# A recommender's attention kernel: four transpose banks, attention as columns, tail chunks spread, one shared PSUM bank

## The chip, the cores and the metric

The kernel runs on one core of a Trainium2 chip. The metric is the device time of one execution in microseconds, as the median of several runs; lower is better. The core has five engines that work side by side and wait for each other by semaphores: TensorE (PE; its weight loads are listed as PEld), VectorE (DVE), ScalarE (ACT), GpSimd (POOL) and SyncE (SP). PE writes its results to PSUM[...].

## The reference: what is computed

For each of 16384 samples, 69 user fields and one label are looked up in a table of 100001 rows of 96 numbers. Each looked-up row `u` gets one attention number from a small network that sees it beside the label's row `q`; the rows, weighted by it, are summed in ten groups of fields; a three-layer network makes one number of the result.

```
u  = emb[batch_user]                      # 16384 x 69 x 96
ql = emb[batch_label[:, 0]]
z  = concatenate([q, u, q - u, q * u])    # q: ql repeated over the fields
h  = dice(z @ W1 + b1, a1)                # 64 hidden numbers
att = (h @ W2 + b2) @ W3 + b3             # one number per sample and field
pre = where(batch_user < 100000, u * att, 0)
pooled = einsum('gf,bfe->bge', window, pre)      # groups of 20,20,10,10,2,2,2,1,1,1 fields
x = concatenate([pooled, ql])
h = dice(bn(x @ Wf1 + bf1)); h = dice(bn(h @ Wf2 + bf2)); return h @ Wf3 + bf3
# dice(x, a) = (a * (1 - p) + p) * x, p = sigmoid(bn(x))
```

All of it is in float32.

## The kernel before

**Tiling.** The samples are cut into 32 blocks (`NBLK`) of 512. A block's lookups are cut into 69 chunks of 512 rows. The first 64 chunks (main chunks) hold eight samples each with their first 64 fields; the last five (tail chunks, `NTAIL`) hold all 512 samples of the block with one field each (65 to 69), whose group sums are trivial. `chunk_of` (L64) says which chunk of which block has the running number c. Two chunks make a pair; there are 1104 pairs (`NPAIR`).

**One pair's way.** `fetch` (L361) gathers eight tiles of 128 rows by indirect DMAs on POOL (`gather`, L267; tile `u`, 17 buffers), turns each by a PE transpose into a PSUM bank `ptr` (pool `ps_tr`, two banks, L250), and DVE makes two copies of it: `uT` (L378), and `quT`, multiplied by the label's row (L381, or L388 for a tail chunk). `hidden` (L391) makes the hidden sums `ph` on PE and their sigmoid `y` on ACT; `product` (L411) finishes the dice on DVE. `attend_rows` (L417), once every four pairs, multiplies the four `y` by `v2` (32 columns, two of them used), each into its own 32 partitions of one bank (`prow`), which ACT copies to `row`; `turn_band` (L433) turns that back with four transposes (`patt`), so that each row of a chunk has its attention on its own partition; `weigh` (L443) makes the weights `rw` of it on DVE. `pool_sums` (L460) multiplies `rw` by the rows `u` on PE into one of three sets in the bank `acc` (L254), and `pool_copy` (L482) brings a set to `pooled` on DVE. A tail chunk has no pool sums: `attend_tail` (L426) multiplies directly.

**Rows that POOL doesn't gather.** One tile of 128 rows in each of 245 chunks is fetched row by row, by direct DMAs on SP's queue (109 chunks, `SP_CHUNKS`) and ACT's queue (136 chunks, `ACT_CHUNKS`), into a ring of seven buffers (`Singles`, L277; issues at L303). `scalar_rows` (L652) puts 16 ACT issues in each pair's step, behind the step's sigmoid.

**The top network.** `top_steps` (L561) cuts a block's top network into ten steps: four parts of the first layer for each of two halves (`top1`, L508), `top2` (L527), `top3` (L536). They have a PSUM bank of their own (`ps_m`, L255).

**Order.** The order is written out by hand (`manual_schedule`, L737): `plan` (L629) lists for step i what is issued, and each engine does its share in that order. In the main loop (L659 to L686) step i holds the hidden sums of pair i-2, 16 ACT row fetches, the pool sums of pair i-9 (`POOL_LAG`, L41), the product of pair i-3, the pooled copy of pair i-10, and then the fetch of pair i; every fourth step also the attention rows, the turning and the weights of four pairs. The last 16 pairs have an order of their own (L688 to L707, L732 to L735). The labels of block n are gathered 14 steps before its first pair, turned 11 and applied 9 steps before (L714 to L716), and the top network of a block starts 13 steps after its last pair (L717 to L719). The pool `ps_x` (two banks) holds `prow`, `patt`, the labels' banks and the tail products.

Of the kernel before, what the change touches and what calls it, by code (L numbers as in the profile page):

```python
# [18 lines left out]
P = 128  # L19
# [21 lines left out]
POOL_LAG = 9  # L41
# [21 lines left out]

def chunk_of(c):  # L64

    n, k = divmod(c, NCH)
    if n == NBLK - 1 and k >= EARLY:
        k = NMAIN + k - EARLY if k < EARLY + NTAIL else k - NTAIL
    return n, k
# [47 lines left out]
def rec_kernel(  # L117
# [132 lines left out]
    ps_tr = ctx.enter_context(tc.tile_pool(name="ps_tr", bufs=2, space=PSUM))  # L250
    ps_h = ctx.enter_context(tc.tile_pool(name="ps_h", bufs=2, space=PSUM))
    ps_x = ctx.enter_context(tc.tile_pool(name="ps_x", bufs=2, space=PSUM))
    ps_acc = ctx.enter_context(tc.tile_pool(name="ps_acc", bufs=1, space=PSUM))
    acc = ps_acc.tile([E, 3, 2, NS, G], F32, tag="acc", name="acc")  # L254
    ps_m = ctx.enter_context(tc.tile_pool(name="ps_m", bufs=1, space=PSUM))  # L255


# [86 lines left out]
    def head_rows(n):  # L344

        for h in range(2):
# [86 lines left out]
    def turn_band(b, n):  # L433

        row = bands.pop(b)
        pt = ps_x.tile([P, 4, n, 32], F32, tag="x", name=f"patt{b}")
        for t in range(4):
            nc.tensor.transpose(  # L438
                pt[:, t].rearrange("p k j -> p (k j)"), row[:, t * P : (t + 1) * P], ident[0 : 32 * n, 0 : 32 * n]
            )  # L440
        turned[b] = pt

    def weigh(b, n):  # L443

        pt = turned.pop(b)
# [14 lines left out]
    def pool_sums(i):  # L460
# [6 lines left out]
        pa = acc[:, i % 3]  # L467
# [75 lines left out]
    def store(n):  # L543

        p4 = ps_x.tile([n, P], F32, tag="x", name="p4")
# [31 lines left out]
    def rows_of(b, n):  # L577
        return lambda: attend_rows(b, n)
# [236 lines left out]
```

## Time and profile before

| | |
|---|---|
| median of 3 runs | 10949.98 us (10947.27 to 10950.51) |
| the profiled execution's own time | 13684.32 us |
| its span, first to last instruction | 13682.6 us |
| mean granted TensorE clock | 0.72 |
| POOL: gathers of `u` + of labels | 8587 + 128, 944 and 946 ns each by their own span |
| DVE `uT` + `quT` (L378, L381) | 673 ns each, x2208 and x2048 |
| ACT copy `row` (L423) | 584 ns, x275 of 128 partitions |
| PE pool sums (L327, `acc`) | x15930 + 454, 269 ns each |
| PE transposes `patt` (L438) | x1108, 375 ns each |
| PE `prow` (L421) | x2208, 851 ns each |
| DMA | 458 MB, 34 GB/s |

The span is that of one execution under the profiler, which is 25% longer than the timed ones. PE's records count each float32 product as two instructions; the durations of overlapping matmuls overlap, so that their sum is more than PE's time. In the prediction's fences a timeline line gives start, duration, engine, line, operation, output and input tiles, count, and in brackets how long the engine sat idle before and what ended that. A group line gives count, busy time and mean, and after the second bar the idle time before the group. "issue" is idle time for which the profile shows no reason, "remote" a semaphore whose setter it can't name.

### The profile page before, as it was taken

What the parts mean: (1) busy time and instruction counts of PE and PEld (TensorE: products, weight loads), DVE (VectorE), ACT (ScalarE), POOL (GpSimd) and SP (SyncE); (2) the same over time, 40 slices, a digit from 0 to 9 for tenths busy, and PEclk for the clock granted to TensorE, in tenths of its full rate; (3) what the DMA queues carried; (4) which work ended last, traced back from release to release, by engine and by line L of the source; (5) the groups of instructions that cost most, each with busy time, mean ns of one, the idle gap of its engine ahead of it and who ended that gap; (6) DMA issues with size and microseconds to landing.
All of it is one profiled execution on the core that took longest, in us unless ns stands there. A gap on an engine that the chain in (4) does not pass through costs nothing.

```text
span 13682.6 us, 171148 instructions
## 1 busy us (share of the span) xinstructions
PE 9106.3 (67%) x41797; PEld 4711.6 (34%) x41797; DVE 5074.9 (37%) x8639; ACT 990.6 (7%) x1657; POOL 8225.3 (60%) x8721
## 2 busy tenths in 40 slices
PE   3666666666666666666776666666666666676668
PEld 1333333333333333333333333333333333333334
DVE  2333333333333333333333333333333333333333
ACT  0000000000000000000000000000000000000001
POOL 5666566656666656666665665665665666556663
PEclk7677776777767777677776777777777777777677
DMA  1111111111111111111111111111111111111111
GB/s 38 34 34 33 34 33 33 33 35 33 33 34 34 35 33 33 33 33 36 33 33 33 33 36 33 34 33 33 36 33 33 34 33 35 33 33 34 33 33 22
DMA packets 344459, 458.45 MB, mean 34 GB/s; under 512 B 202354, under 2 KB 202866, under 8 KB 343330
## 3 DMA queue, kind: packets, MB, share of 16 engines
q0 software_dynamic: 278880, 428.92, 15.0%
q1 hardware_dynamic: 29762, 11.82, 0.4%
q10 hardware_dynamic: 34816, 6.75, 0.3%
q8 instruction: 336, 5.51, 0.2%
q14 instruction: 665, 5.45, 0.1%
HBM read 446.74 MB, written 0.07 MB: 33 GB/s over the span
## 4 chain that ended last, share of the span: by engine, by line
PE 37%; issue 20%; another core or an unknown queue 18%; ACTq 12%; DVE 10%; POOL 2%; ACT 1%; DMA 0%; POOLq 0%
ACTq L303 10%; PE acc L327 8%; PE ph L401 6%; PE ptr L327 6%; PE ph L405 5%; PE p L521 5%; DVE uT L378 3%; DVE quT L381 2%; POOL u L268 2%; PE prow L421 2%; DVE y L415 1%; DVE y L414 1%; ACTq L288 1%; PE pa L430 1%
## 5 line engine op out<-in xcount | busy, mean ns | idle before, releaser
L268 POOL DMA_INDIRECT u<-in_rows,ids x8587 | 8103.5, 944 | 5290.9 <-issue 2228.3
L327 PE MATMUL acc<-rw,u 128*96 128x20 f32 x15930 | 1972.9, 269 | 1685.7 <-issue 1088.5
L489 DVE COPY pooled<-acc 96x160 f32<-96x160 f32 x1008 | 429.0, 426 | 6575.4 <-remote 4728.2
L327 PEld LDWEIGHTS acc<-rw,u 128*96 128x96 f32 x15930 | 1853.6, 201 | 2757.0 <-issue 1954.3
L327 PE MATMUL ptr<-ident,u 128*96 128x128 f32 x8587 | 1655.6, 341 | 866.1 <-issue 659.3
L378 DVE COPY uT<-ptr 96x512 f32<-96x512 f32 x2208 | 1485.9, 673 | 996.2 <-remote 756.4
L405 PE MATMUL ph<-quT,wn 96*64 96x512 f32 x4416 | 1625.1, 727 | 195.2 <-issue 189.6
L401 PE MATMUL ph<-uT,A 128*64 128x512 f32 x4096 | 1637.7, 830 | 156.9 <-issue 106.2
L327 PEld LDWEIGHTS ptr<-ident,u 128*96 128x96 f32 x8587 | 1250.6, 166 | 1082.2 <-issue 864.1
L381 DVE TENSOR_TENSOR quT<-ptr,qT 96x512 f32<-96x512 f32 x2048 | 1378.6, 673 | 0.0
L407 ACT ACTIVATE y<-ph 128x512 f32<-128x512 f32 x1104 | 658.6, 597 | 8853.1 <-remote 3304.5
L405 PEld LDWEIGHTS ph<-quT,wn 96*64 96x64 f32 x4416 | 447.3, 175 | 1257.0 <-issue 1255.2
L414 DVE SCALAR_TENSOR_TENSOR y<-y,na1c,ph 128x512 f32<-128x512 f32 x1104 | 810.3, 734 | 177.1 <-ACT y L407 97.0
L415 DVE SCALAR_TENSOR_TENSOR y<-ph,wn,y 128x512 f32<-128x512 f32 x1104 | 828.8, 751 | 39.4
L521 PE MATMUL p<-pooled,wf 96*100 96x512 f32 (+1 forms) x1400 | 713.8, 643 | 84.9 <-issue 82.0
L438 PE MATMUL patt<-ident,row 128*128 128x128 f32 x1108 | 259.5, 375 | 641.4 <-issue 274.9
L421 PE MATMUL prow<-y,v 128*32 128x512 f32 x2208 | 540.7, 851 | 115.0 <-issue 95.6
L401 PEld LDWEIGHTS ph<-uT,A 128*64 128x64 f32 x4096 | 279.0, 169 | 868.9 <-issue 783.3
L521 PE MATMUL p<-pre,V 96*100 96x512 f32 (+1 forms) x700 | 424.0, 745 | 140.4 <-issue 89.2
L438 PEld LDWEIGHTS patt<-ident,row 128*128 128x128 f32 x1108 | 185.1, 194 | 775.8 <-issue 554.0
L521 PEld LDWEIGHTS p<-pooled,wf 96*100 96x100 f32 x1400 | 251.0, 192 | 450.3 <-issue 450.0
L430 PE MATMUL pa<-y,vrep 64*96 64x512 f32 x320 | 231.3, 895 | 203.2 <-DVE pre L431 127.6
(72 smaller groups left out, 2682.1 us busy)
## 6 DMA issues: line engine op xcount, KB each, us to landing
ring<-in_rows ACTq DMA_DIRECT2D x17408, 0.4 KB
ring<-in_rows SPq DMA_DIRECT2D x13952, 0.4 KB
u<-in_rows,ids POOLq DMA_INDIRECT x8587
ids<-in_idx SPq DMA_DIRECT2D x8, 560.0 KB, 2.5
q<-in_emb,ids POOLq DMA_INDIRECT x128
wf<-in_far SPq DMA_DIRECT2D x1, 1209.0 KB
wn<-in_near SPq DMA_DIRECT2D x1, 236.0 KB, 3.1
ids<-in_idx SPq DMA_DIRECT2D x1, 140.0 KB
```

Source lines behind the costliest of these rows:

```text
L268: nc.gpsimd.indirect_dma_start(out=dst, out_offset=None, in_=table, in_offset=bass.IndirectOffsetOnAxis(ap=index, axis=0),)
L303: d = self.engine.dma_start(out=ring[r : r + 1, b], in_=row_bytes[:, bass.ds(self.values[r], ROW_BYTES)]).then_inc(self.sems[k], 16)
L327: ins = op(out, ring[:, at[0]].bitcast(F32) if at else u[:, 4 * (c % 2) + t, :], other, **how)
L378: nc.vector.tensor_copy(uT[j][0:E], ptr)
L381: nc.vector.tensor_tensor(quT[:, j, :].rearrange("e (s f) -> e s f", f=FM), ptr.rearrange("e (s f) -> e s f", f=FM), by_field(q[:, k * NS ...
L401: nc.tensor.matmul(p, As[n % 2][:, k // 4, :], uT[j], start=True, stop=False)
L405: nc.tensor.matmul(p, Wp, quT[:, j, :], start=False, stop=True)
L407: nc.scalar.activation(y, ph, AF.Sigmoid, scale=S_DICE)
L414: nc.vector.scalar_tensor_tensor(y, y, na1c, ph, ALU.mult, ALU.mult)
L415: nc.vector.scalar_tensor_tensor(y, ph, a1c, y, ALU.mult, ALU.add)
L421: nc.tensor.matmul(pr[32 * k : 32 * (k + 1), :], v2, ys[b + k], start=True, stop=True)
L521: nc.tensor.matmul(p1, w[:, h * DH : (h + 1) * DH], x, start=(k == 0), stop=(k == KTOP - 1))
```

## The change

In the pools: transposes get four banks; `ps_x` has one; the top network's bank `ps_m` goes, and its halves take `ps_x`; one bank `shared` holds two sets of pool sums, the attention columns of five bands of four pairs (`place`), and the last layer's result. In place of rows, copy and turning, `attend` multiplies each quarter of `y`, as the stationary operand, by the two used columns of `v2`: the attention comes out on the right partition at once, and `weigh` reads it from `shared`. The tail chunks of all blocks but the last stand at places 48, 53, 58, 63 and 68 of a block. Pool sums run ten steps behind in place of nine, labels are gathered 16 steps ahead, and the steps of the top network are placed anew.

```diff
-POOL_LAG = 9
+POOL_LAG = 10
...
+TAIL_AT = [48 + 5 * f for f in range(NTAIL)]
 def chunk_of(c):
     n, k = divmod(c, NCH)
-    if n == NBLK - 1 and k >= EARLY:
-        k = NMAIN + k - EARLY if k < EARLY + NTAIL else k - NTAIL
+    if n == NBLK - 1:
+        if k >= EARLY:
+            k = NMAIN + k - EARLY if k < EARLY + NTAIL else k - NTAIL
+    elif k in TAIL_AT:
+        k = NMAIN + TAIL_AT.index(k)
+    else:
+        k -= sum(at < k for at in TAIL_AT)
     return n, k
...
-    ps_tr = ctx.enter_context(tc.tile_pool(name="ps_tr", bufs=2, space=PSUM))
+    ps_tr = ctx.enter_context(tc.tile_pool(name="ps_tr", bufs=4, space=PSUM))
     ps_h = ctx.enter_context(tc.tile_pool(name="ps_h", bufs=2, space=PSUM))
-    ps_x = ctx.enter_context(tc.tile_pool(name="ps_x", bufs=2, space=PSUM))
+    ps_x = ctx.enter_context(tc.tile_pool(name="ps_x", bufs=1, space=PSUM))
     ps_acc = ctx.enter_context(tc.tile_pool(name="ps_acc", bufs=1, space=PSUM))
-    acc = ps_acc.tile([E, 3, 2, NS, G], F32, tag="acc", name="acc")
-    ps_m = ctx.enter_context(tc.tile_pool(name="ps_m", bufs=1, space=PSUM))
+    shared = ps_acc.tile([P, 512], F32, tag="shared", name="shared")
+    sets = shared[0:E, 0:320].rearrange("e (k j s g) -> e k j s g", k=2, j=2, g=G)
+    def place(b, n):
+        start = 320 + 32 * (b // 4 % 5) + 8 * (b % 4)
+        return shared[:, start : start + 8 * n].rearrange("p (t k j) -> p t k j", t=4, j=2)
...
-    def head_rows(n):
-        for h in range(2):
+    def head_rows(n, halves=(0, 1)):
+        for h in halves:
...
-    def attend_rows(b, n):
-        pr = ps_x.tile([P, 512], F32, tag="x", name=f"prow{b}")[0 : 32 * n]
-        for k in range(n):
-            nc.tensor.matmul(pr[32 * k : 32 * (k + 1), :], v2, ys[b + k], start=True, stop=True)
-        row = rpool.tile([P, 512], F32, tag="row", name=f"row{b}")[0 : 32 * n]
-        nc.scalar.copy(row, pr)
-        bands[b] = row
+    def attend(i, b, n):
+        out = place(b, n)
+        for t in range(4):
+            nc.tensor.matmul(out[:, t, i - b, :], ys[i][:, t * P : (t + 1) * P], v2[:, 0:2], start=True, stop=True)
...
-    def turn_band(b, n):
...
     def weigh(b, n):
-        pt = turned.pop(b)
+        pt = place(b, n)
...
-        pa = acc[:, i % 3]
+        pa = sets[:, i % 2]
...
-            banks, tag = (ps_h, "h") if n == NBLK - 1 and cols.start >= BLK // 2 and h == 1 else (ps_m, "m")
+            banks, tag = (ps_tr, "tr") if n == NBLK - 1 and h == 1 else (ps_x, "x")
...
-        p2 = ps_m.tile([D2, BLK], F32, tag="m", name=f"p2_{n}_{cols.start}")[:, cols]
+        p2 = ps_x.tile([D2, BLK], F32, tag="x", name=f"p2_{n}_{cols.start}")[:, cols]
...
-        p3 = ps_m.tile([P, k1 - k0], F32, tag="m", name=f"p3_{n}_{cols.start}")
+        p3 = shared[:, 480 + NQ * (n % 2) + k0 : 480 + NQ * (n % 2) + k1]
...
     for i in range(e):
-        if i >= 7 and i % 4 == 3 and i < e - 1:
-            at(i, rows_of(i - 7, 4))
         if i >= 4:
             at(i, tails_of(i - 4))
-        if i >= 8 and i % 4 == 0:
-            at(i, lambda b=i - 8: turn_band(b, 4))
         if i >= 2:
             at(i, sums_of(i - 2))
         at(i, lambda i=i: scalar_rows(i))
...
+        for k in [i - 5] if i < e - 1 else [i - 5, i - 4]:
+            if k >= 0:
+                at(i, lambda k=k: attend(k, k - k % 4, 4))
         if i >= 3:
             at(i, product_of(i - 3))
...
+        if i < e - 2:
+            if i >= POOL_LAG:
+                at(i, lambda k=i - POOL_LAG: pool_sums(k))
+            if i > POOL_LAG:
+                at(i, lambda k=i - POOL_LAG - 1: pool_copy(k))
...
         at(i, fetch_of(i))
-        if i >= 8 and i % 4 == 0:
-            at(i, lambda b=i - 8: weigh(b, 4))
+        if i >= 9 and (i - 9) % 4 == 0:
+            at(i, lambda b=i - 9: weigh(b, 4))
...
-            at(first - 14, lambda n=n: qs.__setitem__(n, head_gather(n)))
-            at(first - 11, lambda n=n: head_turn(n, qs.pop(n)))
-            at(first - 9, lambda n=n: head_rows(n))
-        if n < NBLK - 2:
-            for s, work in enumerate(top_steps(n, slice(0, BLK))):
-                at(end + POOL_LAG + 4 + s, work)
...
+            at(first - 16, lambda n=n: qs.__setitem__(n, head_gather(n)))
+            at(first - 13, lambda n=n: head_turn(n, qs.pop(n)))
+            at(first - 11, lambda n=n: head_rows(n, [0]))
+            at(first - 9, lambda n=n: head_rows(n, [1]))
+        steps = [12, 12, 13, 13, 15, 15, 16, 16, 18, 20] if n < NBLK - 2 else [12, 12, 12, 12, 13, 13, 13, 13, 18, 19]
+        if n < NBLK - 1:
+            for step, work in zip(steps, top_steps(n, slice(0, BLK))):
+                at(end + step, work)
```

The closing pairs keep their order, with `attend` in the place of the attention rows and without the turning.

More of the change, by code (lines that the diff above doesn't have):

```diff
@@ L431, in attend_tail @@
         nc.vector.scalar_tensor_tensor(pres[n][:, k - NMAIN, :], pa, bb[0:E], uT[j][0:E], ALU.add, ALU.mult)
-    def turn_band(b, n):
[L435 to L441, printed above, removed]
     def weigh(b, n):
-        pt = turned.pop(b)
+        pt = place(b, n)
         rw = rpool.tile([P, 16, 2, 2 * G], F32, tag="rw", name=f"rw{b}")[:, 0 : 4 * n]
@@ L543, in store @@
     def store(n):
-        p4 = ps_x.tile([n, P], F32, tag="x", name="p4")
+        p4 = ps_tr.tile([n, P], F32, tag="tr", name="p4")
         nc.tensor.transpose(p4, res[:, 0:n], ident)
@@ L551, in top3_last @@
     def top3_last(x2):
-        p3 = ps_m.tile([1, P], F32, tag="m", name="p3_last")
+        p3 = ps_x.tile([1, P], F32, tag="x", name="p3_last")
         nc.tensor.matmul(p3, wf3, x2, start=True, stop=True)
@@ L557, in top3_last @@
         nc.sync.dma_start(out=out[B - P :].rearrange("p o -> o p"), in_=r)
-    pooled, pres, x1s, x2s, qs, us, hs, ys, bands, rws, p1s, gates, turned, accs = ({} for _ in range(14))
+    pooled, pres, x1s, x2s, qs, us, hs, ys, rws, p1s, gates, accs = ({} for _ in range(12))
     def top_steps(n, cols):
@@ L577, in rows_of, with work @@
     def rows_of(b, n):
-        return lambda: attend_rows(b, n)
+        def work():
+            for k in range(n):
+                attend(b + k, b, n)
+        return work
     def spread_of(b, n):
-        def work():
-            turn_band(b, n)
-            weigh(b, n)
-        return work
+        return lambda: weigh(b, n)
     def pool_of(k):
@@ L668, in rec_kernel @@
         at(i, lambda i=i: scalar_rows(i))
-        pools = [] if i < POOL_LAG else [i - POOL_LAG]
-        if i == e - 2:
-            pools.append(i - POOL_LAG + 1)
-        elif i == e - 1:
-            pools = [i - POOL_LAG + 1]
-        at(i, *[lambda k=k: pool_sums(k) for k in pools])
+        for k in [i - 5] if i < e - 1 else [i - 5, i - 4]:
+            if k >= 0:
+                at(i, lambda k=k: attend(k, k - k % 4, 4))
         if i >= 3:
             at(i, product_of(i - 3))
-        at(i, *[lambda k=k: pool_copy(k) for k in ([] if i <= POOL_LAG else [i - POOL_LAG - 1, i - POOL_LAG][: 1 + (i == e - 1)])])
-        if i == e - 2:
-            at(i, rows_of(c - 16, 4))
-        elif i == e - 1:
-            at(i, lambda: turn_band(c - 16, 4))
-        at(i, fetch_of(i))
-        if i >= 8 and i % 4 == 0:
-            at(i, lambda b=i - 8: weigh(b, 4))
-        elif i == e - 1:
-            at(i, lambda: weigh(c - 16, 4))
-    at(e, product_of(e - 3), lambda: pool_copy(e - POOL_LAG), tails_of(e - 4))
+        if i < e - 2:
[3 more added lines that the diff above has]
+                at(i, lambda k=i - POOL_LAG - 1: pool_copy(k))
+        else:
+            for k in {2: (-13, -12), 1: (-11, -10)}[e - i]:
+                at(i, lambda k=k: pool_copy(e + k), lambda k=k: pool_sums(e + k + 1))
+        at(i, fetch_of(i))
+        if i >= 9 and (i - 9) % 4 == 0:
+            at(i, lambda b=i - 9: weigh(b, 4))
+        elif i == e - 1:
+            at(i, lambda: weigh(e - 8, 4))
+    at(e, product_of(e - 3), lambda: pool_copy(e - 9), tails_of(e - 4))
     for i in range(e, c):
@@ L713, in rec_kernel @@
                 at(max(0, first - 50), lambda n=n: load_ids(n))
-            at(first - 14, lambda n=n: qs.__setitem__(n, head_gather(n)))
-            at(first - 11, lambda n=n: head_turn(n, qs.pop(n)))
-            at(first - 9, lambda n=n: head_rows(n))
-        if n < NBLK - 2:
-            for s, work in enumerate(top_steps(n, slice(0, BLK))):
-                at(end + POOL_LAG + 4 + s, work)
-        elif n == NBLK - 2:
-            for s, work in enumerate(top_steps(n, slice(0, BLK))):
-                at(end + POOL_LAG + 1 + s // 2, work)
+            at(first - 16, lambda n=n: qs.__setitem__(n, head_gather(n)))
[6 more added lines that the diff above has]
+                at(end + step, work)
     for f in range(NTAIL):
```

## The prediction

> **What bounds the kernel now.** I read the page's busy shares first, then POOL's timeline, then PE's in the same stretches, then what DVE waits for, and last the end of the timeline.
>
> ```profile
> span 13682.6 us, 171148 instructions
> PE 9106.3 (67%) x41797; PEld 4711.6 (34%) x41797; DVE 5074.9 (37%) x8639; ACT 990.6 (7%) x1657; POOL 8225.3 (60%) x8721
> L268 POOL DMA_INDIRECT u<-in_rows,ids x8587 | 8103.5, 944 | 5290.9 <-issue 2228.3
> L489 DVE COPY pooled<-acc 96x160 f32<-96x160 f32 x1008 | 429.0, 426 | 6575.4 <-remote 4728.2
> ```
>
> No engine looks full, and the profiled execution (13684.32 us) is 25% longer than the median (10949.98 us). So the first question is which of these waits exist without the profiler. POOL's timeline at the start, where it has 17 empty buffers and waits for nobody:
>
> ```profile
> 30.25 0.94 POOL L268 DMA_INDIRECT u<-in_rows,ids  x1 [0.30 <-issue]
> 31.50 0.95 POOL L268 DMA_INDIRECT u<-in_rows,ids  x1 [0.30 <-issue]
> ...
> 58.97 0.94 POOL L268 DMA_INDIRECT u<-in_rows,ids  x1 [0.30 <-issue]
> ```
>
> 23 steps in 28.72 us: one gather starts each 1.2487 us. The program has 8587 + 128 = 8715 gathers, the first at 3.27 us. Without a stall the last starts at 3.27 + 8714 x 1.2487 = 10884 us, and that is 99.4% of the median. In the profile it starts at 13556.61: 2672 us of stalls, about 2.4 us a pair of chunks. Now the stretch around one stall, and the same ACT issues at two places:
>
> ```profile
> 11605.23 2.75 PE L327 MATMUL acc<-rw,u 128*96 128x20 f32 x16
> 11607.81 1.92 PE L327 MATMUL ptr<-ident,u 128*96 128x128 f32 x8
> 11614.96 0.42 DVE L489 COPY pooled<-acc 96x160 f32<-96x160 f32 x1 [7.83 <-remote]
> 11615.19 0.94 POOL L268 DMA_INDIRECT u<-in_rows,ids  x1 [2.33 <-remote]
> ...
> 135.34 30.91 ACTq L303 DMA_DIRECT2D ring<-in_rows  x16
> ...
> 219.75 5.08 ACTq L303 DMA_DIRECT2D ring<-in_rows  x16
> ```
>
> The pool sums ended at 11607.98, yet DVE and POOL, which need only their semaphore, go on 7 us later, both at once; and 16 identical issues take 5.08 or 30.91 us. In such stretches everything with many records crawls while POOL, one record each 1.25 us, keeps its pace. I take these delays to belong to the profiled execution. What PE can do where they are rare:
>
> ```profile
> 203.71 1.08 PE L327 MATMUL ptr<-ident,u 128*96 128x128 f32 x8
> ...
> 256.14 1.05 PE L327 MATMUL ptr<-ident,u 128*96 128x128 f32 x8
> ```
>
> Seven pairs in 52.43 us: 7.49 us a pair, with no top net in it. The top net's matmuls (L521 and L532) are busy 713.8 + 424.0 + 104.3 + about 3 = 1245 us, 1.1 us a pair: together 8.6 us. POOL needs 8715 x 1.2487 / 1104 = 9.86 us a pair. So in the timed runs POOL's issue sets the pace, and PE has about 1.2 us a pair to spare and up to 8 pairs of buffered lead.
>
> The end, for what is not POOL:
>
> ```profile
> 13648.10 0.64 PE L327 MATMUL ptr<-ident,u 128*96 128x128 f32 x4
> ```
>
> These are the last transposes; the span ends 34.5 us later. From a gather's start to its transpose pass 2.5 us (17.76 to 20.27 at the start). Outside the span lie 13684.32 - 13682.6 = 1.7 us. Floor: 10884 + 2.5 + 34.5 + 1.7 = **10923 us**. The median lies 27 us above it (0.25%): a few pairs of PE's lag at the end, or short POOL stalls; the profile can't say which.
>
> **What the Trainium skill says.** "Perfetto Trace Analysis", GPSIMD Engine Instruction: a GpSimd instruction's reported span is unreliable, take the start-to-start spacing. I do; the row's 944 ns would have given 8227 us, and POOL would have looked 75% busy. "GPSIMD Engine Reference", Key points: GpSimd shares SBUF interfaces with VectorE, and contends with two-SBUF-input and 2-port instructions. Every large DVE instruction here reads PSUM, before and after, and the spacing is 1.25 us with DVE busy (11603 to 11607) as with DVE idle (30 to 59): nothing moves. "PSUM — Partial Sum Buffer", the section on bank collisions: two engines on one bank and quadrant must be kept apart by semaphores, whatever the addresses. The trace agrees: matmuls into `acc` wait for the pooled copy 113.9 us in total, although three sets rotate. "TensorE: Matmul & The Clock Gate", LDWEIGHTS: a load costs its columns over 1.2 GHz, 107 ns for 128. L540 (weights `x2` of 128 columns, one moving column) is spaced 0.11 us at best and 0.21 us in its slow stretches; the page's price is the lower end.
>
> **The change, part by part.**
>
> *Attention as columns.* Gone, for four pairs: 8 matmuls of `prow` (1.07 us together in a fast stretch, 1.98 in a slow one), 4 transposes `patt` (0.6 to 1.2 us), one ACT copy (0.58 us). That is 0.4 to 0.8 us of PE a pair. Added: 4 products a pair, two PE instructions each as at L540, so 8 x 0.11 = 0.9 to 8 x 0.21 = 1.7 us. Net PE +0.5 to +0.9 us a pair; taking the unlike ends together, +0.1 to +1.3. PE then stands at 8.7 to 9.9, likely 9.2 us a pair, under POOL's 9.86. Cover: POOL's issue. If the cover were gone it would cost 550 to 1000 us. ACT loses 277 x 0.584 = 162 us; per pair ACT has about 5 us of issues, up to 2.2 us of offset loads every second pair and 0.6 of sigmoid, some 7 us: no gain.
>
> *Four transpose banks.* Fewer waits of transposes on `quT` two chunks back: the page shows transposes waiting 60 us for `uT` in all, almost all of it one 60 us wait at the start. Worth at most that, and hidden, as POOL had 17 buffers then.
>
> *Shared bank.* `weigh`'s read now stands in the bank that the next `attend` writes. Behind that `attend` in PE's queue are the pool sums, which already wait for the same `weigh` (617.9 us in this profile), so the wait is moved rather than added; bound 0 to 1 us every fourth pair. Two rotating sets in place of three: no cost, since the bank is taken in turns anyway.
>
> *One `ps_x` bank.* Top-net halves, labels and tail products take it in turn. Steps end+12 to end+20 are the top net, about end+22 to end+26 the next labels, and tails from about end+29: they do not meet. A late release would stop PE for one dice (two ACT and one DVE, about 2.4 us): 0 to 10 us a block, inside the lead.
>
> *Spread tails.* A tail chunk costs about one 512-column product for `Cq` and one for `pa`, and saves 8 pool sums. Five in a row or every fifth chunk is the same sum, smoother; the lead of 8 pairs (8 x 9.86 us) swallows either. Some 60 more small pooled copies, 0.29 us each: 17 us of DVE in all, beside a DVE that is 37% busy.
>
> *Lag 10 for 9, label gathers two steps earlier.* A buffer of 17 is free 7 steps ahead rather than 8. The label gathers pass 16 `u` gathers on POOL's queue; the same 8715 issues. SP's queue is as before.
>
> *The end.* The last two pairs lose prow, row copy, patt (2.5 us from 13657.94 to 13660.47) and gain 16 columns (1.8 us); if PE lags over the last 16 pairs it gains 8 to 14 us. -3 to +14 us, I take -1.
>
> Sum: POOL 0, end -1: 10949, say **10948 us**. In terms of the profiled execution, POOL's own part is the same 10884 us; its further 2672 us of stalls are not carried into the forecast, and its span may move by hundreds of us with PE's records while the time doesn't.
>
> **Rivals.**
>
> 1. *The leftover 27 us is PE's* (stalls at the start, bunched tails, lag at the end), and the change removes it. For: 60 us and 55 us waits at the start. Against: they lie in crawling stretches. Gives the floor, 10923 us or a little under with the shorter end: -0.25%. No version with 8715 gathers at this spacing can do much better.
> 2. *PE takes over*: the columns run at the slow rate of 0.21 us, since they stream almost nothing, and PE, already waiting on `weigh`, passes 9.86 us a pair. Its place is the attend block between the hidden sums and the pool sums. It decides from +1.26 us a pair. At +1.3 plus 0.25 us of bank wait PE stands at 10.15: 1104 x 10.15 + 35 = 11240 us, +2.6%; barely over the edge, 10990. For: PE's granted clock is 0.72, so slow stretches are common. Against: 7.49 already holds slow stretches, and longer PE queues run without gaps.
> 3. *PE's waits are real, not the profiler's*, and PE sets 9.9 us a pair now; then the banks and the smoothing gain until POOL stops them: again 10923. Against: it would be chance that POOL's count gives 99.4% of the time, with three runs within 0.03% of each other.
>
> **How the numbers follow.** Forecast (POOL sets the pace, end unchanged to 20 us) 0.56; rivals 1 and 3 together 0.22; rival 2 0.22. A measurement tells 0.2% (22 us) from no change: faster is under 10928, slower over 10972. The floor is known to some 10 us, so rivals 1 and 3 fall over 0.2% in most cases and the forecast case itself spills a little each way: faster 0.22, same 0.53, slower 0.25. The likeliest case's own range is 10928 to 10972. The range reaches down past the floor to 10915 and up into half of rival 2, 11060.
>
> **What would show it.** POOL's spacing still 1.25 us and 8715 gathers; matmuls 41797 - 2208 - 1108 + 8832 = about 47300; the row copies gone from ACT. Columns spaced 0.11 us speak for the forecast, 0.21 us throughout for rival 2. A time under 10915 would make me wrong about POOL; one over 11000 about PE's slack.

## The result, and the profile after

| | before | after |
|---|---|---|
| median, us | 10949.98 (5 runs, 10947.27 to 10951.21) | 11011.77 (5 runs, 10997.59 to 11014.98) |
| ratio | | 1.0052, 95% interval 1.0040 to 1.0063 |
| the profiled execution's span, us | 13682.6 | 11013.2 |

The kernel is 62 us slower: inside the range that the prediction gave, and on the side to which it gave 0.25. The profile after comes from a chip on which the kernel takes under the profiler what it takes without. The one of before looks like those of a second kind of chip, on which that kernel takes some 13,500 to 13,650 us in timed runs too (below). So a second profile of the unchanged kernel, from a chip of the first kind (run e1), is the partner for comparisons from here on.

The page after, as before: the busy shares, the gathers, the pooled copies; with them the chain of work that ended last, the transposes, the pool sums and the new columns.

```profile
span 11013.2 us, 182668 instructions
...
PE 9871.1 (90%) x47313; PEld 5613.9 (51%) x47313; DVE 5278.4 (48%) x8701; ACT 848.4 (8%) x1380; POOL 8248.5 (75%) x8721
...
POOL 39%; PE 33%; issue 17%; DMA 11%; DVE 1%; ACT 0%; POOLq 0%
...
L282 POOL DMA_INDIRECT u<-in_rows,ids x8587 | 8126.6, 946 | 2619.7 <-issue 2399.4
L341 PE MATMUL ptr<-ident,u 128*96 128x128 f32 x8587 | 2005.4, 361 | 1057.0 <-DMA u<-in_rows,ids 1048.9
...
L435 PEld LDWEIGHTS shared<-v,y 128*128 128x128 f32 x8832 | 1270.1, 222 | 1285.4 <-issue 481.0
...
L490 DVE COPY pooled<-shared 96x160 f32<-96x160 f32 x946 | 404.6, 428 | 3055.5 <-PE shared L341 3011.4
...
L341 PE MATMUL shared<-rw,u 128*96 128x20 f32 x15930 | 1829.7, 260 | 11.8 <-DVE pooled L490 7.1
...
L435 PE MATMUL shared<-v,y 128*128 128x2 f32 x8832 | 1363.0, 276 | 30.8 <-DVE rw L449 23.8
```

POOL's row has the same 8587 gathers; of its 2619.7 us idle, 2399.4 are "issue", the 0.3 us between two gathers. The 5290.9 us of the first profile, and the pooled copies' waits for a "remote" semaphore, are absent in e1 too (2619.4 us, and 2759.3 of 2785.8 us for PE), so the change didn't remove them. The same busy lines of e1, the kernel before on a chip of the first kind, and its transposes' waits:

```profile
span 10932.3 us, 171148 instructions
...
PE 8841.4 (81%) x41797; PEld 4308.0 (39%) x41797; DVE 5266.7 (48%) x8639; ACT 1001.5 (9%) x1657; POOL 8231.5 (75%) x8721
...
L327 PE MATMUL ptr<-ident,u 128*96 128x128 f32 x8587 | 1977.7, 331 | 1934.5 <-DMA u<-in_rows,ids 1913.0
```

POOL is as busy in both, PE 1030 us busier after the change: 0.93 us a pair. Almost everywhere this lies in time in which PE waited before: its transposes wait 1913.0 us for gathered rows in e1 and 1048.9 us after the change. Where it doesn't is seen at the end of the two POOL and PE timelines (start, duration, then the instruction). First the last gathers and the last transposes after the change:

```profile
10908.50 0.95 POOL L282 DMA_INDIRECT u<-in_rows,ids  x1 [0.31 <-issue]
...
10971.42 1.07 PE L341 MATMUL ptr<-ident,u 128*96 128x128 f32 x4
...
10975.55 0.64 PE L341 MATMUL ptr<-ident,u 128*96 128x128 f32 x4
```

And the same two places in the kernel before (e1):

```profile
10891.28 0.94 POOL L268 DMA_INDIRECT u<-in_rows,ids  x1 [0.30 <-issue]
...
10893.33 0.64 PE L327 MATMUL ptr<-ident,u 128*96 128x128 f32 x4
...
10896.43 0.64 PE L327 MATMUL ptr<-ident,u 128*96 128x128 f32 x4
```

I call **tail** the time from the start of the last gather to the end of the span. It is 10932.3 - 10891.28 = 41.0 us before, and 11013.2 - 10908.50 = 104.7 us after: 63.7 us more, which is the loss. From the last transposes to the end the two hardly differ (35.9 and 37.7 us). So PE comes to those transposes with a lag: the data of the last tile were asked for at 10908.50 and turned 67 us later, where before it took 5.

Where does the lag begin? I took for each of the 1104 pairs the shortest time from a gather's start to its transpose. I call this time PE's **lag**. After the change its median is 2.9 us up to pair 1081; it rises to as much as 17 us for a few pairs in many a block and comes down again, and POOL never stalls (none of the 8714 spacings reaches 1.5 us). Then the lag goes 15, 32, 37, 41 us in pairs 1082 to 1085, and ends at 67. PE's timeline there:

```profile
10691.58 1.40 PE L341 MATMUL ptr<-ident,u 128*96 128x128 f32 x6
10693.39 0.45 PE L341 MATMUL ptr<-ident,u 128*96 128x128 f32 x1 [0.41 <-DMA u<-in_rows,ids]
10694.58 0.45 PE L341 MATMUL ptr<-ident,u 128*96 128x128 f32 x1 [0.75 <-DMA u<-in_rows,ids]
10694.83 6.30 PE L522 MATMUL p<-pre,V 96*100 96x512 f32 x10
10700.96 1.02 PE L522 MATMUL p<-qT,wf 96*100 96x512 f32 x2
10701.82 8.75 PE L522 MATMUL p<-pooled,wf 96*100 96x512 f32 x20
...
10713.22 1.05 PE L435 MATMUL shared<-v,y 128*128 128x2 f32 x8
10714.14 1.51 PE L341 MATMUL shared<-rw,u 128*96 128x20 f32 x16
10715.50 1.85 PE L341 MATMUL ptr<-ident,u 128*96 128x128 f32 x8
10717.14 5.39 PE L522 MATMUL p<-pre,V 96*100 96x512 f32 x10
10722.36 1.02 PE L522 MATMUL p<-qT,wf 96*100 96x512 f32 x2
10723.22 8.75 PE L522 MATMUL p<-pooled,wf 96*100 96x512 f32 x20
10734.38 1.09 PE L441 MATMUL pa<-y,vrep 64*96 64x512 f32 x2 [2.42 <-DVE x L505]
...
10742.11 0.51 PE L341 MATMUL ptr<-ident,u 128*96 128x128 f32 x3
```

At 10694 PE still waits for gathers: it is on time. Then block 30's whole first top-network layer stands in two steps (`end + 12` and `end + 13`, four parts each): 15.7 us of matmuls ahead of one pair's transposes, 14.8 ahead of the next. From the last transpose of pair 1081 to the first of pair 1082 pass 20.9 us, and from there to the first of pair 1083 26.6 us, where POOL brings a pair each 10. The kernel before begins this network at `end + 10` and puts two parts into each step (L717 to L719), and its transposes of the same pairs come 12 and 14 us apart:

```profile
10682.32 1.06 PE L327 MATMUL ptr<-ident,u 128*96 128x128 f32 x8
10683.21 4.46 PE L521 MATMUL p<-pre,V 96*100 96x512 f32 x10
10687.50 1.02 PE L521 MATMUL p<-qT,wf 96*100 96x512 f32 x2
10688.36 1.88 PE L521 MATMUL p<-pooled,wf 96*100 96x512 f32 x4
...
10694.28 1.06 PE L327 MATMUL ptr<-ident,u 128*96 128x128 f32 x8
10695.17 7.03 PE L521 MATMUL p<-pooled,wf 96*100 96x512 f32 x16
...
10708.26 0.51 PE L327 MATMUL ptr<-ident,u 128*96 128x128 f32 x3
```

There the lag comes to 26 us in pairs 1084 and 1085, and PE works it off to 5.5 by the end. With the columns it doesn't.

### The profile page after: what moved, and what is told of

It is laid out like the page before. It is cut to its first block, busy times and chain, and to the rows that moved or that the text cites. A ratio compares the mean times of both kernels' runs of the same rounds, so it can differ in the third digit from the quotient of the medians.

```text
span 11013.2 us, 182668 instructions
## 1 busy us (share of the span) xinstructions
PE 9871.1 (90%) x47313; PEld 5613.9 (51%) x47313; DVE 5278.4 (48%) x8701; ACT 848.4 (8%) x1380; POOL 8248.5 (75%) x8721
## 4 chain that ended last, share of the span: by engine, by line
POOL 39%; PE 33%; issue 17%; DMA 11%; DVE 1%; ACT 0%; POOLq 0%
POOL u L282 38%; DMA u<-in_rows,ids 11%; PE p L522 7%; PE shared L341 6%; PE ph L415 5%; PE ptr L341 4%; PE shared L435 4%; PE ph L419 4%; PE pa L441 1%; PE ph L412 1%; POOL q L282 1%; PE ph L417 1%; PE pc L364 0%; PE p L533 0%; PE shared L541 0%
## 5 line engine op out<-in xcount | busy, mean ns | idle before, releaser
L282 POOL DMA_INDIRECT u<-in_rows,ids x8587 | 8126.6, 946 | 2619.7 <-issue 2399.4
L341 PE MATMUL ptr<-ident,u 128*96 128x128 f32 x8587 | 2005.4, 361 | 1057.0 <-DMA u<-in_rows,ids 1048.9
L435 PEld LDWEIGHTS shared<-v,y 128*128 128x128 f32 x8832 | 1270.1, 222 | 1285.4 <-issue 481.0
L415 PE MATMUL ph<-uT,A 128*64 128x512 f32 x4096 | 1903.9, 951 | 3.4 <-DVE y L429 3.4
L490 DVE COPY pooled<-shared 96x160 f32<-96x160 f32 x946 | 404.6, 428 | 3055.5 <-PE shared L341 3011.4
L341 PE MATMUL shared<-rw,u 128*96 128x20 f32 x15930 | 1829.7, 260 | 11.8 <-DVE pooled L490 7.1
L419 PE MATMUL ph<-quT,wn 96*64 96x512 f32 x4416 | 1799.6, 817 | 0.0
L341 PEld LDWEIGHTS shared<-rw,u 128*96 128x96 f32 x15930 | 1745.2, 192 | 22.2 <-DVE pooled L490 8.4
L435 PE MATMUL shared<-v,y 128*128 128x2 f32 x8832 | 1363.0, 276 | 30.8 <-DVE rw L449 23.8
L522 PE MATMUL p<-pooled,wf 96*100 96x512 f32 (+1 forms) x1400 | 609.7, 586 | 0.0
L415 PEld LDWEIGHTS ph<-uT,A 128*64 128x64 f32 x4096 | 298.0, 187 | 443.5 <-issue 362.1
L441 PE MATMUL pa<-y,vrep 64*96 64x512 f32 x320 | 316.9, 1092 | 4.1 <-DVE x L505 2.4
```

The source lines that it names most:

```text
L282: nc.gpsimd.indirect_dma_start(out=dst, out_offset=None, in_=table, in_offset=bass.IndirectOffsetOnAxis(ap=index, axis=0),)
L341: ins = op(out, ring[:, at[0]].bitcast(F32) if at else u[:, 4 * (c % 2) + t, :], other, **how)
L415: nc.tensor.matmul(p, As[n % 2][:, k // 4, :], uT[j], start=True, stop=False)
L419: nc.tensor.matmul(p, Wp, quT[:, j, :], start=False, stop=True)
L435: nc.tensor.matmul(out[:, t, i - b, :], ys[i][:, t * P : (t + 1) * P], v2[:, 0:2], start=True, stop=True)
L441: nc.tensor.matmul(pa, vrep[j * H1 : (j + 1) * H1, :], y[j * H1 : (j + 1) * H1, :], start=True, stop=True)
```

## The experiments

**Theory A**: POOL's issue still sets the pace, the change costs nothing up to pair 1081, and the loss stands wholly in the tail: the lump of block 30's top network, and columns in the last pairs, where PE has no slack. **Rival B**: PE, with its columns, sets the pace throughout. **Rival C**: the waits on shared banks, or the spread tail chunks, cost a little in each block.

Runs e1 to e18 fell on five chips of two kinds. On the first two (e1 to e4, e5 to e8) the kernel before takes 10929 and 10954 us; on the others (e9 to e12, e13 to e15, e16 to e18) 13504, 13648 and 13633. Each chip was used at one time only, so "kind of chip" is a name for what was seen: whether the chip or something else at that time makes the difference, no run shows. A ratio is always to the kernel before on the same chip. Tails are compared on the first kind only; each is that of one execution. The kernel before has 41.0 us in e1, and its versions in e8 and e7, with the same end, have 38.9 and 42.0.

### e1, the kernel before again; e5, the kernel after again

> The kernel before, profiled once more, to see it without the delays of its first profile. If POOL's issue sets the pace in it as in the changed kernel: 8715 gathers spaced 1.2515 us on average with no stall, the last one started at about 10908 us, and some 40 us from there to the end (10949.98 - 1.7 - 10908.5). If PE set its pace: stalls of POOL of over 0.1 us a pair, or gathers spaced well under 1.25 us.

> The changed kernel again, beside the others on one chip. Every theory: its ratio to the kernel before is 1.004 to 1.0063 as at first; the gathers keep their spacing of this chip without a stall, and what it loses stands behind the last gather (85 to 105 us there, against 41 in the kernel before).

e1: 10934.05 us in one run (12 runs of the same kernel on that chip: median 10928.99), tail 41.0 us. e5: 11005.02 us, ratio 1.0051 [1.0038, 1.0065]; its last gather starts at 10888.33 in a span of 10997.7, a tail of 109.4 us. The loss is there on another chip, and again behind the last gather. The gathers themselves have two paces: 1.2495 us from start to start in e1 and 1.2491 in e5, but 1.2515 in the first profile after. Over 8714 steps 1.2515 - 1.2491 is 21 us. The medians mix executions of both paces (e5's five run from 10998.63 to 11021.27 us), so tails are compared rather than times.

### e2, the top network spread

```diff
-        steps = ... if n < NBLK - 2 else [12, 12, 12, 12, 13, 13, 13, 13, 18, 19]
+        steps = ... if n < NBLK - 2 else [12, 12, 13, 13, 14, 14, 15, 15, 17, 18]
-            banks, tag = (ps_tr, "tr") if n == NBLK - 1 and h == 1 else (ps_x, "x")
+            banks, tag = (ps_tr, "tr") if n == NBLK - 2 or n == NBLK - 1 and h == 1 else (ps_x, "x")
```

> The changed kernel, with the top network of block 30 spread over steps end+12 to end+18, two parts a step, in place of four parts a step, and its first-layer sums in the transposes' banks. Theory A (the lump of four parts a step at pairs 1081 and 1082 throws PE some 30 us behind, and the closing pairs give it no chance to catch up): the lag at pair 1085 falls from 41 us to under 20, the time from 11012 to 10965-10985. Theory B (the attention columns leave PE without slack, so any burst near the end stays): the lag only comes two pairs later, the time stays within 10 us of 11012.

10975.70 us, ratio 1.0042 [1.0028, 1.0055]; tail 10976.3 - 10891.05 = 85.3 us: 19 to 24 less than with the lump. The lag builds more slowly (pair 1083: 14 in place of 32 us). At pair 1085 it is 30, where theory A asked for under 20; it reaches 40 and ends at 48. By the tail the lump is about a third of the loss; the ratio alone doesn't show it, since its interval overlaps that of e5. The edit also moves the first-layer sums into the transposes' banks, which no run separates from the spreading.

### e3, half of the column work

Quarters 1 and 3 of each pair's attention are left zero.

```diff
-        for t in range(4):
-            nc.tensor.matmul(out[:, t, i - b, :], ys[i][:, t * P : (t + 1) * P], v2[:, 0:2], start=True, stop=True)
+        for t in range(0, 4, 2):
+            nc.tensor.matmul(out[:, t : t + 2, i - b, :], ys[i][:, t * P : (t + 1) * P], v2[:, 0:4], start=True, stop=True)
```

> The changed kernel with half of the attention's weight loads: quarters 1 and 3 of each pair's attention are left zero, the rest is unchanged. It takes 0.5 us a pair off PE at the full clock, 0.9 at the half clock. Theory A: the jump of the lag at pairs 1082-1085 stays at 25 us or more, and the time falls by 10 to 25 us (22 closing pairs at 0.5 to 0.9 us). Theory B: the lag at the end goes almost wholly, time 10950-10965.

10961.07 us, ratio 1.0027 [1.0016, 1.0039]; last gather at 10889.88, span 10963.0: tail 73.1 us, 32 to 36 less, with the lump still in place (lag 41 us at pair 1085, as after). With half of the columns the lag doesn't grow further (it ends at 42 in place of 67). The jump at pairs 1082 to 1085 stays, as theory A had it, but the gain is more than the 10 to 25 us that A allowed for the loads themselves.

### e4, columns in the kernel before

```diff
-    acc = ps_acc.tile([E, 3, 2, NS, G], F32, tag="acc", name="acc")
+    shared = ps_acc.tile([P, 512], F32, tag="shared", name="shared")
+    sets = shared[0:E, 0:320].rearrange("e (k j s g) -> e k j s g", k=2, j=2, g=G)
...
-        pt = turned.pop(b)
+        pt = place(b, n)
...
-        pa = acc[:, i % 3]
+        pa = sets[:, i % 2]
...
-            at(i, lambda b=i - 8: turn_band(b, 4))
```

`attend` and `place` come as in the change, called where `attend_rows` stood, four pairs at once. Banks, tails, and the top network stay as before.

> The kernel before with the columns alone (and the bank that they share with two sets of pool sums): banks for transposes, places of tail chunks, lag, labels and top network as before. Theory A: the columns alone cost little, 10950 to 10970. Theory B: they alone bring most of the loss, 10995 or more.

10966.46 us, ratio 1.0033 [1.0020, 1.0045]; tail 10965.7 - 10888.04 = 77.7 us, 36.7 more than before. The timeline of its end:

```profile
10888.04 0.94 POOL L275 DMA_INDIRECT u<-in_rows,ids  x1 [0.30 <-issue]
...
10925.20 1.07 PE L334 MATMUL ptr<-ident,u 128*96 128x128 f32 x4
...
10929.81 1.09 PE L334 MATMUL ptr<-ident,u 128*96 128x128 f32 x4
```

Columns and the bank that they share with two sets of pool sums, without the lump and the other parts, cost 37 us, and all behind the last gather (that starts no later than before). That is more than half of the 64 to 68 us, so the run is nearer to what B forecast for it than to A's "cost little" (its time lies in A's range because this chip's kernel before takes 10929 us, not 10950). B's reason, a PE that sets the pace throughout, doesn't show: none of the loss stands ahead of the last gather. Where these 37 us go is read after e6.

### e6, both undone at the end of the kernel after

e2's two edits, and for the last 20 pairs rows, copy and turning (as in the kernel before, in banks of `ps_tr`) in place of columns.

```diff
     def rows_of(b, n):
-            for k in range(n):
-                attend(b + k, b, n)
+        return lambda: attend_rows(b, n)
...
-        return lambda: weigh(b, n)
+            turn_band(b, n)
+            weigh(b, n)
```

> The changed kernel with two undoings, both only near the end: block 30's top network spread as in the second run, and the attention of the last 20 pairs by rows, copy and turning (in transposes' banks) in place of columns. Theory D (the whole loss is PE's lag from pair 1081 on, made by the lump of the top network and by the columns' loads in the last 22 pairs; the 1080 pairs before cost nothing): the lag at the end under 20 us, 40 to 55 us behind the last gather, time within 15 us of the kernel before. Rival R (the single bank for labels, tails and top network and the bank that columns and pool sums share are what holds the closing pairs): the lag at the end stays over 35 us, the time 30 us or more above before.

10971.36 us (21 runs), ratio 1.0016 [1.0009, 1.0022] where the change has 1.0051; tail:

```profile
10888.01 0.94 POOL L282 DMA_INDIRECT u<-in_rows,ids  x1 [0.30 <-issue]
...
10905.51 0.64 PE L341 MATMUL ptr<-ident,u 128*96 128x128 f32 x4
...
10908.56 0.64 PE L341 MATMUL ptr<-ident,u 128*96 128x128 f32 x4
```

10944.5 - 10888.01 = 56.5 us: 48 to 53 of the change's excess are gone, though 1084 of 1104 pairs keep their columns, and all keep the banks and the order. This speaks against B and C as the main cause. 15.5 us of tail are left, and the time agrees: 10971.36 - 10954.27 = 17 us. Each of the three stands a little outside what theory D asked: a lag of 20.9 us at the end for under 20, a tail of 56.5 for 40 to 55, 17 us of time for 15.

**Where the time goes in the closing pairs.** The stretch runs from the first transpose of pair 1085 to the last transpose of all; "idle" is its length less PE's busy time, "clock" the mean granted TensorE clock in it. The hidden sums are the same 152 matmuls in every row.

| | length, us | PE idle | clock | columns, or rows and turning | hidden sums |
|---|---|---|---|---|---|
| e1, before | 157.2 | 19.3 | 0.82 | 12.2 | 47.2 |
| e6 | 166.3 | 18.4 | 0.78 | 13.5 | 48.9 |
| e3 | 179.7 | 23.7 | 0.72 | 12.8 | 51.6 |
| e4 | 193.7 | 21.6 | 0.70 | 28.4 | 55.3 |
| e2 | 196.3 | 23.0 | 0.70 | 25.7 | 57.0 |
| after | 205.4 | 21.7 | 0.66 | 26.3 | 57.2 |

The lines behind the first and the last row give the stretch, its length, the busy time (and instructions) of PE, PEld, DVE, ACT and POOL, and then the clock and the DMA's share and GB/s:

```profile
10739.60:10896.80 157.20, 137.86 (x842) 89.86 (x842) 89.08 (x155) 19.55 (x37) 115.45 (x123) 0.82 0.19 40
...
10770.50:10975.90 205.40, 183.71 (x968) 132.22 (x969) 92.01 (x160) 17.69 (x33) 105.11 (x112) 0.66 0.13 28
```

PE's idle time hardly differs (19.3 and 21.7 us), so waits, those on the shared bank among them, don't make the 48 us between the two. The columns' own time makes some 14 of them. Much of the rest is unchanged work that takes longer at the lower clock: in e4 the hidden sums take 1.17 times what they take in e1, and the clock is lower by the same factor; after the change the factors are 1.21 and 1.24. With the columns the clock falls on one chip (e1 to e4), with rows in their place and the top network spread it rises on another (0.66 in e5, 0.78 in e6). So a column near the end costs more than its own time. Why the clock falls, and whether a fall of it alone would cost as much, no run shows.

### e8, the spread tail chunks alone

```diff
+TAIL_AT = [48 + 5 * f for f in range(NTAIL)]
...
+    elif k in TAIL_AT:
+        k = NMAIN + TAIL_AT.index(k)
+    else:
+        k -= sum(at < k for at in TAIL_AT)
```

> The kernel before with the tail chunks of blocks 0 to 30 spread as in the change, and nothing else. Theory D: no difference beyond 8 us, since it only smooths PE's work before pair 1069, where PE waits for the gathers anyway. If bunched tails cost POOL time: faster by 10 us or more.

10952.13 us, ratio 1.0000 [0.9991, 1.0008]. The prediction's 0 for it holds; of rival C the tails are out.

### e7, fewer gathers in the kernel before

A tile of each seventh pair's second chunk in place of each tenth pair's comes by SP's direct DMAs; POOL has 47 gathers fewer.

```diff
-SP_CHUNKS = [2 * (10 * s + 8) + 1 for s in range(109)]
+SP_CHUNKS = [2 * (7 * s + 8) + 1 for s in range(156)]
```

> The kernel before with a row-by-row chunk on SP in every 7th pair in place of every 10th: 156 chunks for 109, so 47 gathers fewer on POOL and 6016 more direct DMAs on SP (0.32 us each, 41 us a chunk in 69 us). If POOL's issue sets the pace: 47 x 1.2495 = 59 us less. If PE is as much the limit: under 20 us less.

10893.91 us, ratio 0.9945 [0.9931, 0.9958]: 60.4 us gained, where 47 gathers at 1.25 us are 59. POOL's group now:

```profile
L268 POOL DMA_INDIRECT u<-in_rows,ids x8540 | 8083.0, 946 | 2607.8 <-issue 2414.7 <-DMA u<-in_rows,ids 98.6 <-PE ptr L327 69.7
```

The gain per gather is the spacing, to within the measurement: POOL's issue is the bound of the kernel before on this kind of chip. This version beats both kernels.

### e9, e10, e12: POOL out of the way

Four of the eight gathers of each pair are left out, in the kernel before (e9) and after (e10); e12 is e10 with e3's half columns.

```diff
-        ins = op(out, ... u[:, 4 * (c % 2) + t, :], other, **how)
+        ins = op(out, ... u[:, 4 * (c % 2) + t % 2, :], other, **how)
...
-                else:
+                elif t < 2:
```

> The kernel before with POOL's cover taken off: of each chunk only tiles 0 and 1 are gathered (4 gathers a pair, some 5 us of POOL), and tiles 2 and 3 are read from those of 0 and 1; everything else runs as before, on half of the users' rows. The time is then PE's own pace with its waits. The prediction's sum says 8.6 us a pair, 9530 us in all; theory D (PE waits for gathers most of the time) asks for 9600 or less.

> The changed kernel with the same half of the gathers left out. The prediction's sum says 0.5 to 0.9 us a pair more than the kernel before in the same state, 550 to 1000 us; theory D asks that it be under 10900, since its whole run is hidden behind POOL. Rival R (waits on the shared bank) would show as DVE waits on PE and PE waits on DVE grown by more than the loads' own time.

> The same with half of the attention's weight loads too (quarters 1 and 3 of the attention left zero), but all of its turns on the shared bank. If the columns cost by their loads: 400 to 900 us less than with all columns (1104 pairs x 4 loads x 0.1 to 0.2 us). If by the turns on the bank: less than 150 us.

They ran on a chip of the second kind (kernel before 13504 us). e9: 8981.82 us. e10: 9040.54, 59 more. e12: 8777.01, 264 less than e10. The busy lines and the engine shares of the chains that ended last, first of e9:

```profile
PE 7441.3 (83%) x41797; PEld 3970.9 (44%) x41797; DVE 5124.6 (57%) x8639; ACT 980.2 (11%) x1657; POOL 4288.1 (48%) x4550
...
PE 51%; ACTq 24%; issue 14%; DVE 6%; another core or an unknown queue 3%; ACT 2%; DMA 0%; SPq 0%
```

and of e10:

```profile
PE 8584.9 (95%) x47313; PEld 5172.3 (57%) x47313; DVE 5186.0 (58%) x8701; ACT 844.5 (9%) x1380; POOL 4287.7 (48%) x4550
...
PE 81%; ACTq 9%; issue 5%; DVE 3%; another core or an unknown queue 1%; ACT 1%; DMA 0%; SPq 0%
```

With half of the gathers gone, PE does all its work of the kernel after, all top networks included, at 9013.8 / 1104 = 8.2 us a pair, at a mean clock of 0.80. In the profile after, at 0.70, it is busy 9871.1 / 1104 = 8.9 us a pair. Both are under POOL's 9.9, so B is wrong for the run as a whole. PE's idle time falls from 1520 us in e9 to 429 in e10, so longer waits on the shared bank (the rival R named there) don't show either.

The cover that the prediction priced at 550 to 1000 us costs 59 here. The likely reason is that e9 isn't bound by PE alone: ACT's row issues are 24% of its chain, and the columns fill PE's gaps (busy +1144 us, time +59). In e12 ACT's share comes back (29%). Its 264 us lie between what was expected of the loads (400 or more) and of the turns on the bank (under 150), and settle neither.

### e11 and e15, still fewer gathers

SP's rows every 5th and every 6th pair (217 and 181 chunks, 108 and 72 gathers fewer).

> The kernel before with a row-by-row chunk on SP in every 5th pair: 217 chunks, 108 gathers fewer than before. If POOL still sets the pace and SP keeps up (41 us of issues in 49 us): 108 x 1.25 = 135 us less than the kernel before. If SP falls behind or PE becomes the limit: less than 100 us.

> The kernel before with SP's rows every 6th pair: 181 chunks, 72 gathers fewer. SP needs 128 x 0.38 = 49 us for a chunk, and six pairs take 59 us, so it should keep up: -72 x 1.25 = -90 us, 10860 us. If SP or the ring of four buffers comes late at that distance, POOL stalls and the gain is smaller than the 60 us of every 7th pair, or a loss.

e11: 17194.64 us, ratio 1.2726 [1.2707, 1.2746]; e15: 15812.19, ratio 1.1582 [1.1556, 1.1608]. Gains of 135 and 90 us were expected. Both fell on chips of the second kind and say nothing on the first. The chain of e11 names its bound, SP's queue:

```profile
SPq 64%; issue 35%; PE 1%; DVE 0%; DMA 0%; another core or an unknown queue 0%; ACT 0%; ACTq 0%
```

### e13 and e16, e14 and e17, e18: the end and the pace, asked again

e13 is e6 with rows for all pairs from 1044 on; e14 is e6 with e7's edit; e16 and e17 repeat them, e18 is the kernel after.

```diff
+    ROWS_FROM = e - 44
...
-            if k >= 0:
+            if 0 <= k < ROWS_FROM:
```

> The kernel after, with block 30's top network spread and with rows, copy and turning in place of columns for all pairs from 1044 on (not only for the last 20): the last 60 pairs do their attention as the kernel before does. If the columns of pairs 1064 to 1083 are what was left of the loss, the stretch from the start of the last gather to the end falls from 56.5 us to 41 to 46 (the kernel before has 41), and the time to within 5 us of the kernel before at the same gather spacing. If something else is left (two sets of pool sums in place of three, one bank for the top network, the later pool sums), it stays at 52 to 58 us, and the time 12 to 18 us over the kernel before.

> The kernel after with both repairs of its end (top network of block 30 spread, rows for the last 20 pairs) and a single-field chunk of rows on SP's queue every 7th pair: 47 gathers fewer. If POOL's issue sets the pace in the kernel after as in the one before, it gains 47 x 1.25 = 59 us on the repaired kernel, which stood 17 us over the one before: 10950 + 17 - 59 = 10908 us. If PE set the pace of the changed kernel, it gains nothing: 10967 us.

> The same kernel as with rows from pair 1044 on, which fell on a chip where the kernel before takes 13648 us. On a chip where that takes some 10950 us: if the columns of pairs 1064 to 1083 are what was left, the stretch from the start of the last gather to the end is 41 to 46 us and the time within 5 us of the kernel before; if something else is left, 52 to 58 us and 12 to 18 us over it. On a chip of the slower kind the tail can't be read, and the time should again be 1 to 2% under the kernel before.

> The same kernel as the repaired one with SP's rows every 7th pair. On a chip where the kernel before takes some 10950 us: 40 to 45 us under it if POOL's issue sets the pace, about 17 us over it if PE does. On a chip of the slower kind, again some 5% over it, since SP's issues set the pace there.

> The kernel after, unchanged. On a chip where the kernel before takes some 10950 us: 0.5% slower again, with a tail of 105 to 110 us beside the two kernels of the same call. On a chip of the slower kind: 1 to 2% faster than the kernel before, as its version with rows in the last 60 pairs was, if what is slow there is paid per instruction and semaphore of ACT and PE's band steps; 0.5% slower if the end alone makes the difference.

| | us | ratio to the kernel before there |
|---|---|---|
| e13 | 13427.82 | 0.9837 [0.9817, 0.9857] |
| e14 | 14377.79 | 1.0540 [1.0517, 1.0562] |
| e16 | 13435.81 | 0.9853 [0.9826, 0.9880] |
| e17 | 14383.27 | 1.0551 [1.0521, 1.0580] |
| e18, the kernel after | 13482.43 | 0.9891 [0.9863, 0.9918] |

All five fell on chips of the second kind, so the 15 us of tail and the gather count in the changed kernel stay open. Two things follow. On such a chip the change is 1.1% *faster*; why, no run shows. And the end that e16 repairs costs time there too: e16 is 46.6 us under e18 on the same chip (13421.83 to 13456.35 against 13474.77 to 13496.38), and the tail falls from 13486.3 - 13336.21 = 150.1 to 13454.6 - 13327.72 = 126.9 us, where the first profile of the kernel before has 13682.6 - 13556.61 = 126.0. That is half of the gain; where the other half comes from is not shown, so its nearness to e6's 48 to 53 us confirms nothing.

## Why the prediction was wrong, and where it was right

**The step that failed is "The end": -3 to +14 us, taken as -1.** The tail measured +64 to +68 us, the whole loss. The step priced the last two pairs, and the columns' own time over 16 pairs for the case that PE lags. That own time was sized about right: some 14 us more in the closing pairs. The step left three things out.

1. The diff's own line for block 30, `[12, 12, 12, 12, 13, 13, 13, 13, 18, 19]`. The text spoke of "steps end+12 to end+20" of a block only to ask whether two users of one bank meet. For block 30, whose end is followed by 34 pairs, two steps hold 30 us of matmuls; the kernel before began two pairs earlier and had half of that in a step. By the tail of e2 this is 19 to 24 us.
2. With the columns, PE's unchanged work takes longer. In the closing pairs the granted clock is 0.66 in place of 0.82 (0.70 in e4, with the columns and their bank alone), and the same hidden sums take 57.2 us in place of 47.2. So e4 costs 37 us and half of the columns in e3 brings 32 to 36 back, more than their own time in either case.
3. PE's slack of 1.2 us a pair is a mean, and it helps only while gathers are still to come. In e1 PE's transposes wait 1.7 us a pair for gathered rows, and in the profile after still 0.95. After pair 1081 the top network of block 30, the last block's tail chunks and its first quarters of top network come together with nothing behind that could absorb them.

e6, with lump and columns both undone at the end, gains 48 to 53 us, less than the two apart.

What remains of the tail, 15.5 us, isn't settled. About half of it is there at pair 1085 (a lag of 33 us in e6, 26 in e1); the rest comes later, at a clock of 0.78 where e1 has 0.82. The network's start two pairs later, columns in the pairs up to 1083, or two sets of pool sums in place of three may be it. The runs that were to tell (e13, e16) fell on chips of the second kind.

**Right: POOL sets the pace.** The spacing of 1.25 us, the 8715 gathers and the floor held: e7 shows it for the kernel before at 60.4 us for 47 gathers. For the kernel after there are the POOL timeline without a single stall, the 1048.9 us for which PE's transposes still wait for gathers, and e10's 8.2 us a pair. The same gain from fewer gathers was not shown for it (e14, e17).

**Most likely wrong in its cause, harmless in its use: the long profiled execution.** The text put its 2672 us of stalls down to the profiler. On three chips timed runs of the kernel before take 13504 to 13648 us, so such stalls occur without it, and e1 shows a profile without them. On which chip the first profile was taken is not on record. Setting those stalls aside was right for the executions that gave the 10949.98 us.

**The 27 us above the floor, and rival 1.** They look like POOL's: the gather has two paces, 1.249 and 1.2515 to 1.252 us, and the difference is 21 to 26 us over the run. e8, the kernel before but for its tail chunks, took 10951.18 us in its profile, with a mean spacing of 1.2517 us, no stall and a tail of 38.9 us. That speaks against rivals 1 and 3, which gave the 27 us to PE. The kernel before itself was profiled at the shorter pace only.

**PE's sum.** The columns stand 0.115 us apart in a fast stretch (10713.22 to 10714.14 for eight) and 0.216 in a slow one, as priced; over the run they take 1363.0 / 8832 = 0.154 us each. In e1 `prow` and `patt` take 452.5 + 209.7 us, so the change's own sum is +701 us, 0.63 a pair, inside the likely 0.5 to 0.9. PE is 0.93 a pair busier, since other work grew too: a hidden sum of L415 takes 951 ns where in e1 it takes 868, at a mean clock of 0.70 against 0.74. The prediction had no term for that. Its pace of 9.2 us a pair stands beside 8.9 of busy time in the profile after. Matmuls: 47313, which is what the prediction's sum gives; ACT lost 277 copies.

**Rival 2** is right in one thing: PE does run past POOL once the columns are on it. But it does so in the last 22 pairs, not in each attend block, and the columns don't run at the slow rate throughout (0.16 us each in the closing pairs): from the transposes at 10691.58 to those at 10975.55 PE takes 284 us for 22 pairs, 12.9 a pair. "One over 11000" was to mean an error in PE's slack, and that is what it was.

**The costs taken as nothing.** Spread tails: 0 (e8). The four banks, the shared bank and the one `ps_x` bank were not tried one by one; before pair 1081 together they leave no trace on POOL. In the profile after, PE stands idle for 30.8 us before the columns and for 11.8 us before the pool sums, which write the shared bank: 43 us in the whole run. The 113.9 us that the prediction read as waits for the pooled copy belong to the long execution; e1 has 6.0.

## What to carry to other kernels

A mean slack covers added work only while something comes after it to absorb the bursts. Treat the last stretch, in which the pacing engine has done its part, as a kernel of its own, and count each engine's work there pair by pair, with every list of steps that has a special case for the last blocks. Count the unchanged work there too, since it can take longer when work is added: here its time grew with the fall of the granted clock. The tail behind the pacing engine's last instruction is a sharper measure than the whole time: a loss of half a per cent stood out there as 105 us against 41.

## What the hardware showed that was not expected

The direct DMA issues of ACT and SP, the same instructions, vary far more on the second kind of chip than on the first. The summary of the ring tile that the row fetches fill (operation, count, then minimum, median and maximum in ns), first of e1:

```profile
L303 ACTq DMA_DIRECT2D ring<-in_rows x17408: 213/213/535, 18.9 to 10763.0; - x198
```

and of e18, on a chip of the second kind:

```profile
L317 ACTq DMA_DIRECT2D ring<-in_rows x17408: 2/213/1427, 71.8 to 13273.2; - x198
```

The median is the same 213 ns; the longest takes 1.4 us in place of 0.5. A chunk's 128 issues on SP take 48.95 us in e1 and 119.03 us in the first profile of before, read at 5000 us. On chips of the second kind SP's rows cost more the more there are: 13648 us with 109 chunks and 15812 (e15) with 181 on one of them, 17195 (e11) with 217 on another. On the other kind 156 chunks were a gain. What holds the issues up is not shown.

The other surprise is the clock granted to PE. With the columns PE is busy for 90% of the span in place of 81%, and the mean clock is 0.70 in place of 0.74; in the closing pairs it is 0.66 in place of 0.82.
